# The start's norm from centred squares on ScalarE, image edges set to the mean on two engines, and five pieces of background work moved to other steps

## The chip, the cores and the metric

The kernel runs on one core of a Trainium2 chip. The core has TensorE (PE; its weight loads are listed as PEld), VectorE (DVE), ScalarE (ACT), GpSimd (POOL) and SyncE (SP), which here only issues transfers. Each engine works through its own queue in order, and the engines wait for each other by semaphores. The metric is the device time of one execution in microseconds (us).

## The reference

The input is x, four images of 32 x 32 pixels with 16 channels in float32. Four layers follow each other, each of the form x = x + layer(group_norm(x)). The group norm makes eight groups of two channels and takes mean and variance of an image over all pixels of a group, with 1e-5 added to the variance.

```python
def conv(inputs, M, W, G):               # layers 0, 1 and 3
    first = einsum('ijyx,byxc->bijc', M, inputs)
    shifted = conv3x3(inputs, G)         # for each pixel (i, j) its own filters to f channels, zero padding
    diff = relu(inputs[:, None, None, :, :, :] - shifted)   # b, i, j, y, x, f
    second = einsum('ijyx,bijyxf->bijf', W, diff)
    return first - second

def interval(a, W0, b0, W1, b1, W2, b2): # layer 2
    r = concat(running max, running min of a over the intervals i <= j)
    f = max over k of sigmoid(r[i, k] W0a + r[k, j] W0b + b0)
    f = max over k of sigmoid([f, r][i, k] W1a + r[k, j] W1b + b1)
    return sigmoid([f, r] W2 + b2)
```

Nearly all of the work is `shifted`: for each of the 1024 pixels (i, j) and 16 channels, a 3 x 3 convolution of the whole image.

## The kernel before

The images are worked as two groups g of two images b. Three convolution layers by two groups make six phases, and each phase has eight chunks of 128 pixels (i, j), which lie on the partitions. A chunk has 32 steps, one for each filter f and image b: 1536 steps in all. A step makes 128 x 1024 numbers in a pair of PSUM banks, of which there are four.

**A step** (`first_part`, `second_part`). A float32 product is split in parts[...]. `first_part` issues matmuls with the image copies `ib` and `ia`, then ACT scales the pair of banks (L699). `second_part` issues those with `iyz` and `im9` (named `im` in the profile) and then the reduction on DVE (L716, its output is named `junk`): min with 0, product with the chunk's W, sum. The pair of banks is free when L716 has read it. The first 16 steps ("plain") use float32 weights and the image `raw` itself.

**Weights** (`prep_parts`, L217 to L258). The weights of four filters (a unit) are made ready in a cycle of eight steps: L204 on DVE cuts off the low bits; ACT scales the ninth tap (L176), copies (L237, L241); POOL subtracts and adds (L238, L239, L242) and casts (L244, L246), one after the other; then `prep(u + 1)` subtracts the centre from the next unit's weights (L215, POOL). In the last three steps of the cycle SP issues the copies between halves (L252) and loads a later unit (`load_raw`, L111). L204 of the next unit needs the result of L215.

**Work behind the steps** (`behind`, L768). All the rest is written as generators. `conv_layer` (L743) takes one element of `prep_parts` in each step, and when a counter has run out one element of `behind`. A positive yield in `behind` is a number of steps to wait, `IDLE` and `CALM` wait until the weight cycle is in a step marked so; CALM marks the last three steps of the eight. What is emitted in a step goes into the engines' queues at that place, so the yields set the order of each queue by hand. In phase 0 the work behind is: the rest of the first image's start (`rest_of_start`), group 0's norm, the `constants` of the interval layer, then the next phase's input (`before_conv`), and the loads and matmuls of the first terms. In phases 3 and 4 the interval layer of a group runs behind, and then `before_conv` for the last layer.

**The group norm** (`group_norm`, L334) is a row of small DVE operations with `gap` steps between them, POOL for the centred values and squares, and `inverse_root` (L313): three DVE operations on integers (L319 to L323), then 13 small POOL operations (L326, and three rounds of L328 to L331) and the product with the centred values (L376).

**Placing** (`place`, L291). `split` cuts the image in high and low parts in `temp`. From there SP copies quarters of the partitions into `ia` (eight transfers per image) and `ib` (four).

**The start** (L793 to L903). The first phase's images are loaded as rows shifted by taps (`raw`, slots 0 to 2), not normalised. `XQ` holds the same image with a quarter of the pixels of one channel on each partition. DVE sums it (L842), a matmul makes the group's mean for each row (`to_own`), DVE subtracts it (L856), squares and sums (L859), and a matmul gives the variance. ACT takes the root, DVE the reciprocal (L870). `normal` then normalises slots of `raw` on DVE (L890) or ACT (L887, L888), after which `sides` (L873) multiplies the edges, which lie outside of the image, with 0 or 1 (`kept`); in slot 2 a memset clears the column past the image. `prep_plain` subtracts the centre from the first weights (L215, DVE).

## Time and profile before

| | us |
|---|---|
| median of 3 runs (2476.86 to 2479.35) | 2479.14 |
| the profiled execution | 2478.91 |
| its span | 2477.1 |
| PE busy | 2457.9 |
| DVE busy | 2077.0 |
| ACT busy | 1871.4 |
| POOL busy | 1589.7 |
| ACT scaling, L699, one | 1.008 |
| DVE reduction, L716, one | 1.224 |
| first matmul of the first step begins | 9.61 |

In the profile a line such as "L716 DVE ... junk<-pc,WT 128x1024 f32 x1536 | 1879.6, 1224 | 353.5 <-PE pc L663" gives the source line, the engine, what is written from what, the count, then the busy time of all, the mean of one in ns, and the idle time of the engine ahead of them with what ended it. A line of the list in time begins with start and duration in us; a bracket at its end is the idle time of the engine just before and what ended that. TensorE's granted clock was 1.000 in the profiled execution.

### The profile page before, as it was taken

Reading aid. Unit: us, or ns where it says so; the run is one execution under the profiler, and the core shown is the slowest. Engines: PE = TensorE matmul, PEld = TensorE weight load, DVE = VectorE, ACT = ScalarE, POOL = GpSimd, SP = SyncE. Lnnn points to the kernel's source line nnn. Section 1 sums busy time; section 2 is a strip of 40 time slices with the busy share of each in tenths; the row PEclk is TensorE's granted clock in tenths of the full one; section 3 lists DMA queues with packets and bytes.
Section 4 is the critical chain, followed back from the end, with each engine's and each line's share of the span. In section 5 each row is a group of like instructions: output and inputs, shape, how many; then the busy total and the mean of one; then the engine's idle time right before and its main releaser. Section 6 shows DMA issues by size and latency. Waiting matters only on the chain. (4 is left out here: it accounts for less than half of the span.)

```text
span 2477.1 us, 58166 instructions
## 1 busy us (share of the span) xinstructions
PE 2457.9 (99%) x21906; PEld 2072.9 (84%) x21906; DVE 2077.0 (84%) x3637; ACT 1871.4 (76%) x2159; POOL 1589.7 (64%) x1857
## 2 busy tenths in 40 slices
PE   8999999999999999999999999999999999999999
PEld 5998888888888888888888898888889888888887
DVE  9888878888888888878888888888888888788887
ACT  3778767787777778767777777777777787677776
POOL 4767545676565667555567776776777675555552
PEclk9999999999999999999999999999999999999999
DMA  6457654475444467644454454674445476554442
GB/s 198 128 156 191 188 144 134 131 195 149 135 142 137 137 168 194 190 112 136 137 145 129 126 142 132 174 171 130 129 135 141 119 197 186 154 148 137 137 137 54
DMA packets 97674, 366.92 MB, mean 148 GB/s; under 512 B 26480, under 2 KB 31472, under 8 KB 97392
## 3 DMA queue, kind: packets, MB, share of 16 engines
q1 hardware_dynamic: 96832, 362.79, 53.5%
q8 instruction: 172, 2.82, 0.5%
q14 instruction: 110, 0.90, 0.1%
q10 hardware_dynamic: 432, 0.39, 0.0%
q0 software_dynamic: 128, 0.02, 0.0%
HBM read 199.78 MB, written 1.02 MB: 81 GB/s over the span
## 5 line engine op out<-in xcount | busy, mean ns | idle before, releaser
L716 DVE SCALAR_TENSOR_TENSOR junk<-pc,WT 128x1024 f32<-128x1024 f32 x1536 | 1879.6, 1224 | 353.5 <-PE pc L663 303.8
L699 ACT ACTIVATE pc<-pc 128x1024 f32<-128x1024 f32 x1520 | 1532.2, 1008 | 563.8 <-PE pc L663 530.4
L663 PE MATMUL pc<-ib,parts 64*128 64x512 f32 x6080 | 950.2, 388 | 4.3 <-DVE junk L716 3.0
L663 PE MATMUL pc<-iyz,parts 64*128 64x512 f32 x6080 | 947.2, 387 | 2.3 <-ACT pc L699 1.6
L663 PE MATMUL pc<-ia,parts 64*128 64x496 f32 x6080 | 924.8, 379 | 0.0
L663 PEld LDWEIGHTS pc<-ib,parts 64*128 64x128 f32 x6080 | 582.4, 184 | 109.8 <-DVE junk L716 9.6
L663 PEld LDWEIGHTS pc<-ia,parts 64*128 64x128 f32 x6080 | 585.4, 184 | 106.0
L663 PEld LDWEIGHTS pc<-iyz,parts 64*128 64x128 f32 x6080 | 583.5, 184 | 92.6 <-ACT pc L699 7.3
L663 PE MATMUL pc<-im,W 64*128 64x496 f32 x3072 | 603.2, 384 | 0.0
L238 POOL TENSOR_TENSOR parts<-raw,upper_w 128x512 fp32r<-128x512 f32 x190 | 247.0, 1300 | 497.6 <-DVE upper_w L204 413.1
L663 PEld LDWEIGHTS pc<-im,W 64*128 64x128 f32 x3072 | 296.6, 184 | 56.9 <-issue 3.4
L244 POOL CAST parts<-parts 32x512 fp32r<-32x512 f32 x380 | 231.6, 609 | 39.3 <-ACT parts L241 20.8
L242 POOL TENSOR_TENSOR parts<-parts 128x512 fp32r<-128x512 f32 x190 | 247.0, 1300 | 1.6 <-ACT parts L237 1.5
L246 POOL CAST parts<-upper_w 32x512 fp32r<-32x512 f32 x380 | 233.1, 613 | 22.8
L239 POOL TENSOR_TENSOR W<-W,raw 128x512 fp32r<-128x512 f32 x190 | 247.4, 1302 | 0.4 <-ACT W L176 0.3
L215 POOL TENSOR_TENSOR raw<-raw,ident 128x512 f32<-128x512 f32 x190 | 199.8, 1052 | 73.7 <-DMA raw<-in_g 45.8
L176 ACT ACTIVATE W<-raw,low_w 128x512 fp32r<-128x512 f32 x190 | 136.2, 717 | 1.7 <-DMA raw<-in_g 1.6
L716 DVE DVE_READ_ACCUMULATOR junk<-pc,WT 128x1 f32 x1536 | 127.9, 83 | 0.0
L237 ACT ACTIVATE parts<-upper_w 128x512 fp32r<-128x512 f32 x190 | 118.9, 626 | 7.7 <-DVE upper_w L204 7.5
L241 ACT CAST parts<-upper_w 128x512 fp32r<-128x512 f32 x190 | 116.4, 613 | 0.0
L731 POOL TENSOR_SCALAR acc<-acc 128x32 f32<-128x32 f32 x40 | 15.6, 391 | 136.8 <-DVE junk L716 134.7
L204 DVE TENSOR_SCALAR upper_w<-raw 128x512 int32<-128x512 int32 x190 | 82.4, 433 | 19.0 <-POOL raw L215 18.6
(152 smaller groups left out, 470.4 us busy)
## 6 DMA issues: line engine op xcount, KB each, us to landing
raw<-in_g SPq DMA_DIRECT2D x190, 768.0 KB, 7.1
parts<-parts SPq DMA_DIRECT2D x380, 384.0 KB, 5.0
WT<-in_w SPq DMA_DIRECT2D x48, 512.0 KB, 4.7
MT<-in_mt SPq DMA_DIRECT2D x24, 512.0 KB, 7.3
raw<-xs SPq DMA_DIRECT2D x120, 71.8 KB, 4.1
ib<-temp SPq DMA_DIRECT2D x40, 128.0 KB, 4.4
ia<-temp SPq DMA_DIRECT2D x80, 62.0 KB, 5.6
ib<-first SPq DMA_DIRECT2D x8, 128.0 KB, 2.4
```

Of the source, the lines that this page charges most:

```text
L176: nc.scalar.activation(dst, src, AF.Copy, scale=mask[:, 1:2])
L215: eng.tensor_tensor(raws[u][:, s, at:to], raws[u][:, s, at:to], pick[s][:, f0 + at : f0 + to].unsqueeze(2).to_broadcast([P, to - at, P]), ...
L237: nc.scalar.activation(WD, high, AF.Copy, scale=-EPS)
L238: nc.gpsimd.tensor_tensor(WL, w8, high, ALU.subtract)
L239: nc.gpsimd.tensor_tensor(W9, W9.bitcast(F32), src[:, 2], ALU.add)
L241: nc.scalar.copy(WU, high)
L242: nc.gpsimd.tensor_tensor(WD, WD.bitcast(F32), WL.bitcast(F32), ALU.add)
L244: nc.gpsimd.tensor_copy(WU[hi], WL[lo].bitcast(F32))
L246: nc.gpsimd.tensor_copy(WL[lo], high[hi])
L663: nc.tensor.matmul(ps[:, h, at : at + n], lhsT=w[r], rhs=v[r] if n == NH else v[r][:, :n], start=first and k == 0, stop=k == len(pairs) - ...
L699: nc.scalar.activation(ps, ps, AF.Copy, scale=1.0 + EPS)
L716: nc.vector.scalar_tensor_tensor(junk, ps.rearrange("p h n -> p (h n)"), 0.0, chunks[n], op0=ALU.min, op1=ALU.mult, accum_out=accs[phase][ ...
```

## The change

- **Statistics at the start.** The squares are taken on ACT (`Square` with the bias minus the partition's own mean, and a running sum), and the difference between the own and the group's mean is corrected afterwards (`off`, `off2`). `Square` and `Sqrt` are in two table sets of ACT.
- **Edges.** The edges are set to the mean ahead of the normalisation (times `kept`, plus `fill`, which is the mean or 0), which makes them 0 afterwards. Those of slots 1 and 2 and the centres of the first weights are on POOL, those of slot 0 on DVE. Slot 2 of the second image is normalised on ACT.
- **Placing** copies `ib` first (four transfers), and `ia` with both halves s in one transfer (four). In `before_conv` it follows the differences and `halve_rest`, with other yields.
- **Constants** begin six steps later instead of one, wait four steps after the memset of `rt`, and yield after each block.
- **Interval norm**: gap 1 for 2, a pause until CALM ahead of `inverse_root`, and 4 steps after it for 6.
- **A yield of 2** stands between the second dynamic step ("b") and the left side l2.

```diff
@@ -210,13 +210,16 @@
             return
+        for s in range(2 if u < PLAIN else 1):
+            minus_center(eng, u, s, at, to)
+
+    def minus_center(eng, u, s, at, to):
         f0 = u % NU * FU
-        for s in range(2 if u < PLAIN else 1):
-            eng.tensor_tensor(
-                raws[u][:, s, at:to], raws[u][:, s, at:to],
-                pick[s][:, f0 + at : f0 + to].unsqueeze(2).to_broadcast([P, to - at, P]),
-                ALU.subtract,
-            )
+        eng.tensor_tensor(
+            raws[u][:, s, at:to], raws[u][:, s, at:to],
+            pick[s][:, f0 + at : f0 + to].unsqueeze(2).to_broadcast([P, to - at, P]),
+            ALU.subtract,
+        )
@@ -257,11 +260,14 @@
-    def prep_plain(u, at=0, to=FU, eng=nc.gpsimd):
-        if at == 0:
+    def plain_unit(u):
+        if u not in units:
             units[u] = [None] * 3 + [
...
             ]
+
+    def prep_plain(u, at=0, to=FU, eng=nc.gpsimd):
+        plain_unit(u)
         prep(u, at, to, eng)
@@ -290,15 +296,17 @@
-        ty, tz = (v.bitcast(F32) for v in halves(temp, b))
+        parts = halves(temp.bitcast(F32)[:, :TEMP], b)
         da, db = (v[g].bitcast(F32)[:, :, b] for v in (ia, ib))
+        for lo, hi in QUARTERS:
+            for to, src in zip((lo, hi), parts):
+                nc.sync.dma_start(db[to], src[hi])
         for h, (lo, hi) in enumerate(QUARTERS):
-            for s in range(2):
-                at = HW if s == h else 0
-                for to, src in ((lo, ty), (hi, tz)):
-                    nc.sync.dma_start(da[to, s, :LAST], src[lo, s, at : at + LAST])
-            for to, src in ((lo, ty), (hi, tz)):
-                nc.sync.dma_start(db[to], src[hi])
+            for k, to in enumerate((lo, hi)):
+                at = (2 * k * GB + b) * NH + HW * (1 - h)
+                pitch = GB * NH + HW * (2 * h - 1)
+                src = temp.bitcast(F32)[lo, at : at + 2 * pitch].rearrange("p (s n) -> p s n", s=2)
+                nc.sync.dma_start(da[to, :, :LAST], src[:, :, :LAST])
         yield 1
@@ -331,7 +339,7 @@
-    def group_norm(g, name, dst, gap):
+    def group_norm(g, name, dst, gap, pause=None, behind=6):
@@ -372,9 +380,11 @@
         v = yield from totals(f"v{name}")
+        if pause is not None:
+            yield pause
         rstd = inverse_root(v, name)
         nc.gpsimd.tensor_tensor(pair_view(dst), pair_view(xc), spread(rstd), ALU.mult)
-        yield 6
+        yield behind
@@ -409,17 +419,18 @@
         yield 6 if layer == 2 else 12
-        temp = big.tile([P, 8192], F32R, tag="big", name=f"temp_{g}{layer}")[:, :TEMP]
+        temp = big.tile([P, 8192], F32R, tag="big", name=f"temp_{g}{layer}")
         for b in range(GB):
...
             halve(image(im9[g][:, b], HW), image(raw[:, 2, b], WP), low_x)
-            yield from place(g, b, temp)
             for s in range(2):
                 difference(nc.gpsimd, g, b, s, temp)
+            yield 2
+            halve_rest(image(im9[g][:, b], HW), image(raw[:, 2, b], WP), low_x)
+            yield 2
+            yield from place(g, b, temp)
             yield 1
-            halve_rest(image(im9[g][:, b], HW), image(raw[:, 2, b], WP), low_x)
-            yield 4
@@ -481,7 +492,7 @@
         nc.gpsimd.memset(rt, 0.0)
-        yield 1
+        yield 4
@@ -496,8 +507,8 @@
                 blocks(t[:, q * GB : (q + 1) * GB, :], k, mask2, GB)
+                yield 1
             iv[name] = t.rearrange("p k c -> p (k c)")
-            yield 1
     def interval_layer(g):
@@ -523,7 +534,7 @@
         nc.gpsimd.memset(r[:R, H:], 0.0)
-        yield from group_norm(g, f"i{g}", xi, 2)
+        yield from group_norm(g, f"i{g}", xi, 1, CALM, 4)
@@ -638,6 +649,7 @@
         yield from step("b", ftp, bv[:, 1:2])
+        yield 2
         z = left("l2", iv["f2"])
@@ -772,7 +784,7 @@
             zeros(1)
-            yield 1
+            yield 6
             yield from constants()
@@ -820,66 +832,82 @@
     }
+    beyond = const.tile([P, len(outside)], F32, name="beyond")
     kept = const.tile([P, len(outside)], F32, name="kept")
+    fill = const.tile([P, GB, len(outside)], F32, name="fill")
     keep = {}
     for k, (name, view) in enumerate(outside.items()):
-        keep[name] = kept[:, k : k + 1]
-        nc.vector.tensor_reduce(keep[name], view, axis=AX.X, op=ALU.add)
-    nc.vector.tensor_scalar(kept, kept, -1.0, 1.0, op0=ALU.mult, op1=ALU.add)
+        keep[name] = k
+        nc.vector.tensor_reduce(beyond[:, k : k + 1], view, axis=AX.X, op=ALU.add)
+    nc.vector.tensor_scalar(kept, beyond, -1.0, 1.0, op0=ALU.mult, op1=ALU.add)
     s1 = const.tile([P, 1], F32, name="s1")
-    def first_stats(src, name):
+    def first_stats(by_batch, name):
         ps = bank(f"ps_{name}")
-        by_batch = work.tile([P, GB], F32, tag="by_batch", name=f"by_batch_{name}")
-        nc.vector.tensor_scalar_mul(by_batch, own, src)
         nc.tensor.matmul(
...
+    low_w = rows_mask("low_w", ident.rearrange("p (h w k) -> p w h k", h=2, w=2)[:, 1:2])
+
+    low_p = const.tile([P, 2], F32, name="low_p")
+    nc.vector.tensor_scalar_mul(low_p, low_w, 1.0 / EPS)
+
+    n_own = XQ.shape[1]
     nc.vector.tensor_reduce(s1, XQ, axis=AX.X, op=ALU.add)
+    minus_own = const.tile([P, 1], F32, name="minus_own")
+    nc.vector.tensor_scalar_mul(minus_own, s1, -1.0 / n_own)
+    by_mean = work.tile([P, GB], F32, tag="by_batch", bufs=2, name="by_batch_m0")
+    nc.vector.tensor_scalar_mul(by_mean, own, s1)
     ps = bank("ps_own")
...
     )
-    m = first_stats(s1, "m0")
-    low_w = rows_mask("low_w", ident.rearrange("p (h w k) -> p w h k", h=2, w=2)[:, 1:2])
-    low_x = rows_mask("low_x", ident.rearrange("p (g x k) -> p x g k", g=4, x=2)[:, 1:2])
-    nc.vector.tensor_scalar_mul(low_x, low_x, EPS)
-
-    low_p = const.tile([P, 2], F32, name="low_p")
-    nc.vector.tensor_scalar_mul(low_p, low_w, 1.0 / EPS)
-    mean_own = const.tile([P, 1], F32, name="mean_own")
-    nc.vector.tensor_copy(mean_own, ps[:, :1])
-    nc.vector.tensor_scalar_sub(XQ, XQ, mean_own)
+    m = first_stats(by_mean, "m0")
+    squares = const.tile([P, 256], F32, name="squares")
     s2 = const.tile([P, 1], F32, name="s2")
-    squares = const.tile([P, 256], F32, name="squares")
+    nc.scalar.activation(squares, XQ, AF.Square, bias=minus_own, accum_out=s2)
+
+    plain_unit(0)
+    halve(units[0][3][:, :F0], raws[0][:, 2, :F0], low_p)
+    minus_center(nc.gpsimd, 0, 0, 0, F0)
+    off = const.tile([P, 1], F32, name="off")
+    nc.vector.tensor_tensor(off, minus_own, ps[:, :1], ALU.add)
+    off2 = const.tile([P, 1], F32, name="off2")
     nc.vector.scalar_tensor_tensor(
-        squares, XQ, 1.0, XQ, op0=ALU.mult, op1=ALU.mult, accum_out=s2
+        off2, off, float(n_own), off, op0=ALU.mult, op1=ALU.mult
     )
+    by_var = work.tile([P, GB], F32, tag="by_batch", bufs=2, name="by_batch_v0")
+    nc.vector.scalar_tensor_tensor(
+        by_var, off2.to_broadcast([P, GB]), s2, own, op0=ALU.add, op1=ALU.mult
+    )
+    var = first_stats(by_var, "v0")
     mean0 = const.tile([P, GB], F32, name="mean0")
     minus_mean0 = const.tile([P, GB], F32, name="minus_mean0")
-    var = first_stats(s2, "v0")
     nc.vector.tensor_copy(mean0, m)
     nc.vector.tensor_scalar_mul(minus_mean0, m, -1.0)
+    for b in range(GB):
+        nc.vector.tensor_scalar_mul(fill[:, b], beyond, mean0[:, b : b + 1])
     rstd0 = const.tile([P, GB], F32, name="rstd0")
     nc.scalar.activation(rstd0, var, AF.Sqrt, bias=eps)
-    prep_plain(0, 0, F0, nc.vector)
-    nc.vector.reciprocal(rstd0, rstd0)
-
     def sides(eng, b, slot):
...
         if slot == 2:
-            eng.memset(v[64:, :, HW - 1 : HW], 0.0)
+            at = v[64:, :, HW - 1]
+            eng.tensor_scalar(at, at, mean0[64:, b : b + 1], None, op0=ALU.add)
         for side, at in (
...
             if f"{side}{slot}" in keep:
-                eng.tensor_scalar_mul(at, at, keep[f"{side}{slot}"])
+                k = keep[f"{side}{slot}"]
+                eng.tensor_scalar(
+                    at, at, kept[:, k : k + 1], fill[:, b, k : k + 1], op0=ALU.mult, op1=ALU.add
+                )
@@ -891,14 +919,18 @@
+    sides(nc.vector, 0, 0)
+    sides(nc.gpsimd, 0, 2)
+    minus_center(nc.gpsimd, 0, 1, 0, F0)
+    sides(nc.gpsimd, 0, 1)
+    nc.vector.reciprocal(rstd0, rstd0)
     normal(nc.scalar, 0, 2)
     normal(nc.vector, 0, 0)
-    sides(nc.vector, 0, 0)
+    low_x = rows_mask("low_x", ident.rearrange("p (g x k) -> p x g k", g=4, x=2)[:, 1:2])
+    nc.vector.tensor_scalar_mul(low_x, low_x, EPS)
+    halve(image(im9[0][:, 0], HW), image(raw[:, 2, 0], WP), low_x)
+    normal(nc.vector, 0, 1)
     prep_plain_rest(0, 0, F0)
-    normal(nc.vector, 0, 1)
-    sides(nc.vector, 0, 1)
-    sides(nc.gpsimd, 0, 2)
-    halve(image(im9[0][:, 0], HW), image(raw[:, 2, 0], WP), low_x)
     halve_rest(image(im9[0][:, 0], HW), image(raw[:, 2, 0], WP), low_x)
@@ -908,9 +940,10 @@
         prep_plain_rest(0, F0, FU)
-        for slot in (0, 1, 2):
-            normal(nc.vector, 1, slot)
-            sides(nc.vector, 1, slot)
+        for eng, slot in ((nc.gpsimd, 2), (nc.gpsimd, 1), (nc.vector, 0)):
+            sides(eng, 1, slot)
+        for eng, slot in ((nc.scalar, 2), (nc.vector, 0), (nc.vector, 1)):
+            normal(eng, 1, slot)
         halve(image(im9[0][:, 1], HW), image(raw[:, 2, 1], WP), low_x)
@@ -918,7 +951,7 @@
         yield 2
-        temp = first.bitcast(F32R)[:, used : used + TEMP]
+        temp = first.bitcast(F32R)[:, used:]
         for b in range(GB):
```

A tile of padding is also 48 columns wide instead of 88, and `halves` cuts `temp` to its length itself.

More of the change, by code (lines that the diff above doesn't have):

```diff
@@ L128, in net_kernel @@
     raw = const.tile([P, 3, GB, PITCH], F32, name="raw")
-    const.tile([P, 88], F32, name="pad_parts")
+    const.tile([P, 48], F32, name="pad_parts")
     F0 = 2
@@ L271, in halves @@
     def halves(temp, b):
-        v = temp.rearrange("p (k s b n) -> p k s b n", k=2, s=2, b=GB)
+        v = temp[:, :TEMP].rearrange("p (k s b n) -> p k s b n", k=2, s=2, b=GB)
         return v[:, 0, :, b], v[:, 1, :, b]
```

## The prediction

> **What bounds the kernel now.** I read the totals and the groups by line first, then the list of instructions in time around every place where TensorE (PE) pauses. The totals:

> ```profile
> PE 2457.9 (99%) x21906; PEld 2072.9 (84%) x21906; DVE 2077.0 (84%) x3637; ACT 1871.4 (76%) x2159; POOL 1589.7 (64%) x1857
> ...
> L716 DVE SCALAR_TENSOR_TENSOR junk<-pc,WT 128x1024 f32<-128x1024 f32 x1536 | 1879.6, 1224 | 353.5 <-PE pc L663 303.8
> L215 POOL TENSOR_TENSOR raw<-raw,ident 128x512 f32<-128x512 f32 x190 | 199.8, 1052 | 73.7 <-DMA raw<-in_g 45.8
> L204 DVE TENSOR_SCALAR upper_w<-raw 128x512 int32<-128x512 int32 x190 | 82.4, 433 | 19.0 <-POOL raw L215 18.6
> ```

> PE sets the end: 1536 steps, 1.567 us each (the last matmul of three steps in a row starts at 1562.71, 1564.27 and 1565.84). Nothing in the change alters the matmuls of a step, so it can move only the time at which the first begins and the pauses between steps. Listing the start of the last matmul of each step, I find pauses beyond that pace in some forty places. The change touches few of them, so the forecast is a sum of microseconds.

> How a pause arises is seen at the norm of group 0 before the last layer:

> ```profile
> 1554.90 0.50 POOL L326 TENSOR_SCALAR root_a_c<-root_a_c 128x16 f32<-128x16 f32 x1
> ...
> 1559.87 1.29 POOL L238 TENSOR_TENSOR parts<-raw,upper_w 128x512 fp32r<-128x512 f32 x1
> ...
> 1566.42 1.04 POOL L215 TENSOR_TENSOR raw<-raw,ident 128x512 f32<-128x512 f32 x1
> ...
> 1567.49 0.43 DVE L204 TENSOR_SCALAR upper_w<-raw 128x512 int32<-128x512 int32 x1 [1.38 <-POOL raw L215]
> ```

> The inverse root (Newton: 13 small POOL operations and a product) holds POOL 4.97 us from 1554.90. The weight unit's own POOL work then takes 7.59 us (L238 at 1559.87 to L215's end at 1567.46; 1276.82 to 1284.42 is the same 7.6). DVE's L204 for the next unit waits for L215, and behind it on DVE are queued the reductions L716 that free PSUM. I call lag the start of L716 minus the start of that step's last matmul: about 0.5 on a quiet step, falling 0.2 per step when DVE catches up. Here it peaks at 2.0 and PE loses 0.06. Peaks of 3.83, 3.40 and 2.27 go with losses of 1.49, 1.09 and 0.34. So a loss is the peak less 1.95 to 2.3: that is what four PSUM bank pairs cover.

> The same mechanism, and two others, in the places that the change touches:

> ```profile
> 9.61 3.82 PE L663 MATMUL pc<-raw,first 64*128 64x512 f32 x8 [2.40 <-DVE raw L882]
> 51.14 0.70 PE L663 MATMUL pc<-ib,parts 64*128 64x512 f32 x3 [0.96 <-DMA ib<-first]
> 114.09 0.45 DVE L204 TENSOR_SCALAR upper_w<-raw 128x512 int32<-128x512 int32 x1 [2.41 <-POOL raw L215]
> 1284.45 0.43 DVE L204 TENSOR_SCALAR upper_w<-raw 128x512 int32<-128x512 int32 x1 [2.49 <-POOL raw L215]
> 1643.95 1.04 POOL L215 TENSOR_TENSOR raw<-raw,ident 128x512 f32<-128x512 f32 x1 [7.36 <-DMA raw<-in_g]
> ```

> The first matmul waits for DVE's edges; step 19 waits for the transfer into ib; the other three are late L215s, because of the constants, of the interval norm's Newton, and of a weight load queued on SP behind placing transfers.

> [...] The change needs one more switch, for Square. [...] pairs of matmuls start 0.85 apart until about 14.5 us, 0.43 later[...]. [...] in the trace 128x512 takes 1.05 on POOL (L215), and 128x256 takes 0.41 on DVE and 0.67 on POOL (L376).

> **The change part by part**, against the profiled execution's own 2478.91.

> Start. Now: XQ lands at 3.70, s1 3.72, the subtraction 5.39, squares 5.78 to 6.21, by_batch 6.33, matmul 6.62, rstd on ACT 7.24, reciprocal 7.91, normalise 8.11, edges 8.72 to 9.54, first matmul 9.61. After: Square on ACT needs its table after 3.72, so 5.00; 128x256 on ACT takes about 0.6 (L176 of that size: 0.50), so 5.6; by_var 5.9, matmul 6.2 to 6.5; the W9 product (0.5) and the second table load (1.28) on ACT run to 7.3 and now end last; sqrt 0.26, reciprocal 0.16, normalise 0.58: first matmul at 8.4. Edges and centres run beside this on DVE and POOL; on POOL they end about 9.3, before slot 1 is used. Gain 1.2[...]; both ends 0.5 and 1.2, I take 1.0. [...]

> Small pauses at steps 5 (0.37, DVE normalising image 1, now shared out) and 130 (0.39, placing): 0.76, ends 0 and 0.76; I take it all.

> Placing: 8 transfers for 12, ib first. At 0.6 us of SP per issue, four fewer are 2.4 us, and ib goes four issues sooner where PE waits for it: step 19's 1.25 goes (ends 0.6 and 1.25). ia is now last, but PE wants it 0.45 us after ib in each step. In phase 3 the second image's placing moves from step 1001 to 1009, behind the weight load that it held up (its load was issued at 1633.69, behind twelve placings from 1619.23): steps 1018 and 1019's 1.88 go. It is then still 15 steps ahead of its first use, 23 us.

> Constants: one POOL burst per block becomes one per step: step 59's 1.36 goes. The delay of 14 steps moves all that follows in phase 0, its 8 MT loads on SP and the first terms (7.27 us of PE) too; these only change places, as phase 0 has 256 steps and they end near step 210. But the norm now meets the weight cycle elsewhere, below.

> Interval norms: the pause puts Newton behind L215, in the three steps where POOL has nothing of the weights. Each image lost 1.93 there (1.09 at the Newton, the rest in DVE's backlog with the transposes, which stay and with gap 1 come closer together). Gain 1.1 each, ends 0.5 and 1.7: 2.2.

> The two-step yield after the second step: the matmul ps_l for l2 waits for the transfer of s_b into tables. PE loses 1.56 and 1.68 there and 0.83 for a ps_l that doesn't wait: 0.73 + 0.85 = 1.58 gained. Two steps are 3.1 us, more than the wait.

> Sum of gains: 1.0 + 0.76 + 1.25 + 1.88 + 1.36 + 2.2 + 1.58 = 10.0.

> What is moved, and pays. The yield shifts the next norm (group_norm of layer 2, no pause) by two steps. The order of DVE's instructions after the change shows it: L204 used to follow the root at once; now L204, two L716, the root, six L716, the transpose xt, the next L204. So Newton starts just before L238, and L238 to L215 stand behind it: 12.6 us from Newton's start to L215's end (4.97 + 7.59), with only 6 steps (9.4 us) to the next L204. From the trace: the wait at 1567.49 had a lag of 2.0; Newton starts 2 steps (3.13) later, and 0.42 more because L204 now stands ahead of the root: 2.0 + 3.13 + 0.42 = 5.5, so a loss of 3.25 to 3.6. I take 3.4, and there are two such norms: 6.8. The constants' 14 steps do the same to the norm of group 1 in phase 0: before, its Newton (158.22) stood after the unit's casts and L204 waited only 0.51; now the root comes two L716 after L204, as above. With gap 4 DVE's backlog at the root is 1.2 or so smaller: lag 4.2, loss 1.9 to 2.25, I take 2.1. Sum of losses 8.9. Their cover would be a Newton that ends before L238, and there is none.

> Net: 10.0 - 8.9 = 1.1 faster, 2477.8 on the profiled run's scale. The median shown is 0.23 above that run: forecast 2478.0. About 0.2% (5 us) is what a measurement of this kernel can tell from no change, so the likeliest outcome is no difference.

> **The rivals.**
> One: the late Newtons bite half or not at all. For it: L204 waited 1.80 after the first norm's Newton and PE lost only 0.68. Against: 12.6 us don't fit in 9.4, and the order of both queues is fixed. Time: 2478.0 less 4.5 to 8.9, 2469.1 to 2473.5.
> Two, slower than before: [...]
> Three: the change does less than it says: DVE's closer backlog eats the interval norms' gain (2.2), or the transfers still land late (up to 3.1). Time: 2480 to 2483.

> **How the numbers follow.** The forecast's case 0.55, its own range 2475.5 to 2480 from the ends above; rival one 0.27; rival two 0.06; rival three 0.12. Most of rival one lies below 2474.2, 0.2% under the median; little of two and three lies above 2484.1. So faster 0.27, same 0.67, slower 0.06. The range of 2470.0 to 2482.0 leaves about one in ten on each side.

> **What would show it.** Right: L204 waits of 3.5 or more for L215 near the roots of the last layer's two norms and of group 1 in phase 0, with PE 3 us and 2 us late after them; none near 114, 1284 and 1645; first matmul near 8.4 with two table loads ahead of it; no PE wait for ib at step 19. Wrong: those waits under 2 us, a first matmul after 9.6, or a PE wait for ia at a phase's first step.

## The result, and the profile after

The changed kernel takes 2492.91 us (median of 6, 2491.35 to 2493.68) against 2478.55 before: a ratio of 1.0057 (95% interval 1.0044 to 1.0070), so it is slower by 0.6%. The forecast was 2478.0 and no difference. The gains came as forecast in sum; what the moved work costs was put at 8.9 us and is 23 us.

The totals and the groups that answer to those shown of the kernel before. L728, L218 and L204 are the reduction, the centre of the weights and the cut of their low bits:

```profile
PE 2465.4 (99%) x21906; PEld 2082.3 (84%) x21906; DVE 2076.9 (83%) x3626; ACT 1875.0 (75%) x2164; POOL 1595.3 (64%) x1868
...
L728 DVE SCALAR_TENSOR_TENSOR junk<-pc,WT 128x1024 f32<-128x1024 f32 x1536 | 1879.5, 1224 | 357.5 <-PE pc L675 303.5
...
L218 POOL TENSOR_TENSOR raw<-raw,ident 128x512 f32<-128x512 f32 x190 | 198.0, 1042 | 64.4 <-DMA raw<-in_g 33.0
...
L204 DVE TENSOR_SCALAR upper_w<-raw 128x512 int32<-128x512 int32 x190 | 86.0, 452 | 26.7 <-POOL raw L218 26.0
```

PE is busy 7.5 us longer with the same matmuls, so some of them ran slower; and DVE's idle time ahead of L204 for L218 is 26.0 us instead of 18.6, although the waits near 114, 1284 and 1645 are gone.

Listing the start of each step's last pair of matmuls as in the prediction, I get these differences. They add to 13.9 us; the span grew by 13.6 (2477.1 to 2490.7), and the rest lies in pauses of under 0.2.

| where | lost before | lost after | difference | forecast |
|---|---|---|---|---|
| up to step 16 | (46.42) | (46.08) | -0.34 | -1.37 |
| steps 19, 20 (ib before, ACT after) | 1.29 | 0.56 | -0.73 | -1.25 |
| steps 59 to 63 (constants) | 1.42 | 0 | -1.42 | -1.36 |
| interval norms, 795 to 802 and 1051 to 1058 | 3.90 | 0.48 | -3.42 | -2.2 |
| l2 matmuls, both | 3.24 | 1.68 | -1.56 | -1.58 |
| 1018, 1019 (placing) | 1.88 | 0 | -1.88 | -1.88 |
| 107, 108 (Newton, group 1 of phase 0) | 0 | 3.72 | +3.72 | +2.1 |
| 75, and 130 to 150 | 0.39 | 1.87 | +1.48 | -0.39 |
| 963 to 973 and 1219 to 1228 (last layer's Newtons) | 0.72 | 10.15 | +9.43 | +6.8 |
| 983 to 996 and 1247 to 1252 | 0 | 8.67 | +8.67 | none |

(Up to step 16 the time of the last matmul stands instead of a loss.) L204's wait at group 1's norm is 3.22 us, a little under the 3.5 that the prediction named; PE stops for 1.83 after it.

The list in time at the first of the last layer's norms, to be read against the four lines of the prediction:

```profile
1558.21 0.25 POOL L334 TENSOR_SCALAR root_a_c<-root_a_c 128x16 f32<-128x16 f32 x1 [4.19 <-DVE root_t_c L328]
...
1562.91 1.30 POOL L241 TENSOR_TENSOR parts<-raw,upper_w 128x512 fp32r<-128x512 f32 x1
...
1569.48 1.04 POOL L218 TENSOR_TENSOR raw<-raw,ident 128x512 f32<-128x512 f32 x1
...
1570.55 0.43 DVE L204 TENSOR_SCALAR upper_w<-raw 128x512 int32<-128x512 int32 x1 [3.89 <-POOL raw L218]
...
1572.17 0.72 PE L675 MATMUL pc<-ib,parts 64*128 64x512 f32 x4 [2.95 <-DVE junk L728]
...
1574.11 1.06 PE L675 MATMUL pc<-ib,parts 64*128 64x512 f32 x4
```

This is the forecast stall: 12.31 us from Newton's start to L218's end (12.6 forecast), L204 3.89 late, PE stopped for 2.95. What was not forecast is the last line: the same four matmuls that take 0.62 take 1.06. The windows around it (stretch, its length, busy time of PE, PEld, DVE, ACT and POOL, then the granted clock, the DMA share and GB/s):

```profile
1570.00:1572.00 2.00, 0.00 (x0) 0.00 (x0) 1.45 (x2) 0.99 (x2) 1.41 (x2) 1.00 0.78 160
1572.00:1574.00 2.00, 1.82 (x14) 1.54 (x16) 1.73 (x5) 1.70 (x3) 2.00 (x3) 0.89 0.92 237
1574.00:1576.00 2.00, 2.00 (x12) 1.57 (x12) 1.87 (x3) 0.40 (x1) 1.88 (x3) 0.50 0.88 243
1576.00:1578.00 2.00, 2.00 (x16) 1.59 (x16) 0.93 (x3) 1.01 (x1) 1.43 (x3) 0.75 0.88 192
1578.00:1580.00 2.00, 2.00 (x22) 1.64 (x20) 1.64 (x3) 1.27 (x2) 0.48 (x1) 1.00 0.22 28
```

After the pause the granted clock is at 0.50 from 1573.57 to 1576.99, and PE, now the slow one, loses more (1.38 in step 972 alone, when the lag was down to 1.28). The second stall is 23 steps later. SP's queue and what waits for it:

```profile
1570.64 1.14 SPq L111 DMA_DIRECT2D raw<-in_g  x1
1571.83 7.87 SPq L406 DMA_DIRECT2D xs<-xt  x8
...
1588.57 10.77 SPq L417 DMA_DIRECT2D raw<-xs  x14
...
1600.71 1.20 SPq L111 DMA_DIRECT2D raw<-in_g  x1
...
1610.81 1.04 POOL L218 TENSOR_TENSOR raw<-raw,ident 128x512 f32<-128x512 f32 x1 [5.96 <-DMA parts<-parts]
...
1611.88 1.41 DVE L204 TENSOR_SCALAR upper_w<-raw 128x512 int32<-128x512 int32 x1 [2.83 <-POOL raw L218]
```

The image on its way to the next layer's input goes out as eight transfers `xs<-xt` and comes back as 24 `raw<-xs`. Here the eight stand right behind a weight load and take SP 7.87 us; before, they stood ahead of the copies and the load and took 3.78. The gathers follow late, then the weight load of 1600.71; it landed at 1610.68, and POOL and DVE waited for it. (The view names the copies `parts<-parts` as what ended POOL's wait, but these landed at 1605.04 and 1612.32. The load landed 0.13 before L218 began, as at the other waits of L218 here.) PE's two pauses that follow are also followed by a clock of 0.50, from 1614.54 to 1617.95.

Of the 8.67 in the table's last row, 0.47 is at step 983, where PE waits for the copies `parts<-parts`. The kernel without the two-step yield, below, has 0.33 there, so this small part is not of the second stall.

At the start, the change did what it says:

```profile
4.04 1.28 ACT L872 ACT_TABLE_LOAD   x1 [4.04 <-DMA XQ<-in_xq]
...
5.33 0.51 ACT L872 ACTIVATE squares<-XQ,minus_own 128x256 f32<-128x256 f32 x1
...
6.35 1.28 ACT L895 ACT_TABLE_LOAD   x1
...
7.65 0.26 ACT L895 ACTIVATE rstd<-ps_v,eps 128x2 f32<-128x2 f32 x1
...
8.91 2.08 PE L675 MATMUL pc<-raw,first 64*128 64x512 f32 x4 [2.08 <-issue]
```

Each table load takes 1.28, the next activate begins 0.01 to 0.02 later, and the second load began 0.02 after the activate before it. It was the same in the kernel before at 330.10: the activate ahead of L445's load ended at 330.08, the load took 1.28, and the next activate began at 331.39. So these switches cost 1.28 each and, but for the 0.01 to 0.02 on either side, nothing more that shows.

### The profile page after: what moved, and what is told of

Its sections match the earlier page's. It is cut to its first block, busy times and chain, and to the rows that moved or that the text cites. A ratio compares the mean times of both kernels' runs of the same rounds, so it can differ in the third digit from the quotient of the medians.

```text
span 2490.7 us, 58101 instructions
## 1 busy us (share of the span) xinstructions
PE 2465.4 (99%) x21906; PEld 2082.3 (84%) x21906; DVE 2076.9 (83%) x3626; ACT 1875.0 (75%) x2164; POOL 1595.3 (64%) x1868
## 4 chain that ended last, share of the span: by engine, by line
PE 92%; DMA 2%; DVE 2%; POOL 2%; issue 1%; ACT 1%; DVEq 0%; POOLq 0%; ACTq 0%; SPq 0%
PE pc L675 91%; DMA raw<-in_g 2%; DVE junk L728 2%; PE pf L450 1%; ACT pc L711 1%; DMA first<-in_g 0%; POOL raw L218 0%; DMA parts<-parts 0%; POOL parts L241 0%; POOL parts L245 0%; ACT temp L291 0%; POOL parts L249 0%; POOL parts L247 0%; PE ps_l L584 0%; PE ps_r L599 0%
## 5 line engine op out<-in xcount | busy, mean ns | idle before, releaser
L728 DVE SCALAR_TENSOR_TENSOR junk<-pc,WT 128x1024 f32<-128x1024 f32 x1536 | 1879.5, 1224 | 357.5 <-PE pc L675 303.5
L218 POOL TENSOR_TENSOR raw<-raw,ident 128x512 f32<-128x512 f32 x190 | 198.0, 1042 | 64.4 <-DMA raw<-in_g 33.0
L176 ACT ACTIVATE W<-raw,low_w 128x512 fp32r<-128x512 f32 x190 | 136.2, 717 | 4.8 <-DMA raw<-in_g 4.7
L728 DVE DVE_READ_ACCUMULATOR junk<-pc,WT 128x1 f32 x1536 | 127.7, 83 | 0.0
L204 DVE TENSOR_SCALAR upper_w<-raw 128x512 int32<-128x512 int32 x190 | 86.0, 452 | 26.7 <-POOL raw L218 26.0
```

The costliest lines, as they stand in the source:

```text
L176: nc.scalar.activation(dst, src, AF.Copy, scale=mask[:, 1:2])
L218: eng.tensor_tensor(raws[u][:, s, at:to], raws[u][:, s, at:to], pick[s][:, f0 + at : f0 + to].unsqueeze(2).to_broadcast([P, to - at, P]), ...
L728: nc.vector.scalar_tensor_tensor(junk, ps.rearrange("p h n -> p (h n)"), 0.0, chunks[n], op0=ALU.min, op1=ALU.mult, accum_out=accs[phase][ ...
```

## The experiments

### Taking the two-step yield out of the changed kernel

```diff
         yield from step("b", ftp, bv[:, 1:2])
-        yield 2
         z = left("l2", iv["f2"])
```

> The changed kernel without the two-step yield after the second dynamic step. The changed kernel loses, in each of the last layer's two norms, about 5 us after the late Newton (steps 971 to 973 and 1227 to 1228) and about 4 us some 23 steps later (994 to 996 and 1250 to 1252). Theory A, the shift alone does both, by putting Newton ahead of the weights' POOL work and the image gathers ahead of a weight load on SP: both go, 18.1 us less, and 1.6 us come back at the l2 matmuls: about 2476.4 us. Theory B, the second stall belongs to the new order of placing: only the first goes, about 2484.5 us.

Measured: 2477.44 us, ratio to the kernel before 0.9997 (0.9988 to 1.0005). The list of steps has neither stall of the last layer's norms (steps 963 and 971 lose 0.33 and 0.14, 994 and 1250 nothing) and 1.65 and 1.70 at the l2 matmuls. Theory A holds: one line of two steps costs the changed kernel 15.5 us. The new placing, which is still in, does not make the second stall by itself.

### The two-step yield alone in the kernel before

> The kernel before with the two-step yield alone. The l2 matmuls gain 1.6 us. Theory two stalls from one line: the first stall of 5.1 us comes in both norms, and a second one 20 to 30 steps later, of 4 us or so, in place of the old 1.9 at 1018: about 2493 us. Theory one stall: 2486.5 us. If the shift were harmless: 2477 us.

Measured: 2494.53 us, ratio 1.0057 (1.0037 to 1.0076). In the profiled execution steps 964 to 973 lose 5.24 and 1221 to 1228 5.00 (L204 waits behind Newton, PE stops for 3.3 twice), and 983 to 1003 and 1242 to 1259 lose 4.9 and 3.6 (without the 0.4 of steps 1002 and 1258, which the kernel before has too). So this line has both stalls without any other part of the change, and by itself makes up the slowdown of the whole.

### One Newton round for three, every queue's order kept

```diff
-        for _ in range(3):
+        for _ in range(1 if name in ("c02", "c12") else 3):
```

> The changed kernel with one Newton round instead of three in the two norms ahead of the last layer (it leaves out two thirds of the root's iteration, 8 POOL operations of about 0.31 us, 2.5 us), and with the order of every queue as it is. The first stall's lag falls from 5.0 to about 2.5, its loss from 5.1 to about 0.7 us, with no slow clock. Theory follow-up (the stall 23 steps later comes of the first one): it goes as well, about 2476 us in all. Theory gathers (14 image gathers ahead of a weight load on SP are enough): the stalls of 4 us at 994 and 1250 stay, about 2484 us.

Measured: 2486.59 us in one execution. The first stall went as forecast: the lag peaks at 2.68 and 0.74 is lost at 971, 0.71 at 1227. The second stayed: 4.1 us at 994 to 1003, 5.5 at 1239 to 1259 (again without that 0.4). L204 near 1609 still waits 3.37 for L218. So the second stall does not come of the first. But that the number of gathers sets it, as the expectation named it, is refuted by the next two kernels. In this trace the eight `xs<-xt` are issued 1.2 us behind the weight load of 1569.11, which landed at 1578.01; the first of them lands at 1578.59, 8.3 us after its issue, and the last at 1579.95. In the kernel before they land 1.6 to 1.9 us after their issues.

### Newton in the quiet part in every norm ahead of a convolution

```diff
-        yield from group_norm(g, f"c{g}{layer}", xn, 1 if layer == 2 else 4)
+        yield from group_norm(g, f"c{g}{layer}", xn, 1 if layer == 2 else 4, CALM, 4)
```

> The changed kernel with the pause until CALM (and 4 steps after) in the norms ahead of the convolutions too, so that their Newton stands behind L218; the two-step yield stays. The stalls at 107 to 108 (3.7 us), 971 to 973 (5.1) and 1227 to 1228 (5.1) go in every theory: 13.9 less. Theory A1, the stall 23 steps later is set by how many image gathers SP issues between two weight loads (14 there, 16 here): it stays, about 2479 us. Theory A2, it follows from the first stall, which made SP's transfers late: it goes too, about 2471 us.

Measured: 2471.11 us, ratio 0.9967 (0.9957 to 0.9976): faster than both kernels. The list in time at the same norm:

```profile
1556.56 1.04 POOL L218 TENSOR_TENSOR raw<-raw,ident 128x512 f32<-128x512 f32 x1
...
1557.72 1.14 SPq L111 DMA_DIRECT2D raw<-in_g  x1
...
1558.65 0.25 POOL L334 TENSOR_SCALAR root_a_c<-root_a_c 128x16 f32<-128x16 f32 x1 [1.04 <-DVE root_t_c L328]
...
1561.19 0.42 DVE L204 TENSOR_SCALAR upper_w<-raw 128x512 int32<-128x512 int32 x1
...
1564.51 4.37 SPq L406 DMA_DIRECT2D xs<-xt  x8
```

Newton now runs behind L218, L204 doesn't wait, and no step from 952 to 993 loses anything. All the Newton stalls are gone (107, 971, 1227), and 994 and 1250 lose 0.37 and 0.38, with 16 gathers between two weight loads where the changed kernel has 14. So the count is not what makes the loads late. Here too the eight `xs<-xt` come after a weight load in SP's order, but 6.8 us after it (it landed at 1564.74), and they land 1.9 to 2.4 us after their issues. The edit has two parts, the pause and 4 steps for 6; the next kernel has the second part alone, in the last layer's norms.

### The eight transfers ahead of the weight load

The changed kernel with 4 steps instead of 6 behind the norm of layer 2 and nothing else.

> The changed kernel with 4 steps instead of 6 after the norm ahead of the last layer, so that the eight transfers xs<-xt stand ahead of the weights' copies and load on SP again, as in the kernel before; Newton stays where the change put it. In the changed kernel they stand 1.2 us behind a weight load and land after 5 to 8 us instead of 2. Theory xs (this is what makes the loads some 20 steps later late): the stalls at 994 and 1250 (4.0 and 4.2 us) go, those at 971 and 1227 stay: about 2484.5 us. Theory Newton alone: all stalls stay, 2493 us.

Measured: 2485.14 us, ratio 1.0021 (1.0013 to 1.0030).

```profile
1564.77 3.79 SPq L406 DMA_DIRECT2D xs<-xt  x8
...
1570.29 1.04 POOL L218 TENSOR_TENSOR raw<-raw,ident 128x512 f32<-128x512 f32 x1
...
1571.36 0.43 DVE L204 TENSOR_SCALAR upper_w<-raw 128x512 int32<-128x512 int32 x1 [4.13 <-POOL raw L218]
...
1571.39 1.20 SPq L111 DMA_DIRECT2D raw<-in_g  x1
...
1572.99 0.73 PE L675 MATMUL pc<-ib,parts 64*128 64x512 f32 x4 [2.92 <-DVE junk L728]
```

The first stall is as in the changed kernel (4.81 at 971 and 972, 4.85 at 1227 to 1229); of the second, 0.42 at 996 is left and nothing at 1250. This and the last two kernels part the two stalls: the first is Newton ahead of the weights on POOL, and the second comes with the order on SP that has the eight small transfers close behind a weight load.

One thing is not parted. When the eight move, the gathers move too: 14 and then 10 of them stand between weight loads before and here, 10 and then 14 in the kernels with the second stall, 6, 16 and 2 in the one with the quiet Newtons. The stall goes with how late one weight load is. Counted in steps of the same trace, it is issued at 986.8 to 987.1 in the kernels with the full stall (changed, one round, constants as before, two-step yield alone) and at 983.3 to 985.6 in those without (before, no yield, quiet Newtons, this one). With all norms quiet, below, it is issued at 986.1, and 0.83 is lost at 994 and 995. (At the second norm it is 1243.1 to 1243.5 against 1239.4 to 1242.2.) The late landing of the eight fits as a part of that: in the changed kernel and in the one with quiet Newtons they are issued at the same step, 970.6 and 970.4, and the first gather follows at 974.8 and at 974.0. How much the gathers' own place adds was not tried.

### The constants as before

> The changed kernel with the constants as before (begin after one step, one yield after the memset, none inside the blocks). If the 14 steps of delay put group 1's Newton of phase 0 in the way, the stalls at 107 to 108 (3.7 us) and the added loss at 130 to 150 (1.3 us) go, and step 59's 1.4 us comes back: about 2489.3 us. If the constants' place has nothing to do with it, only step 59 comes back: about 2494.3 us.

Measured: 2489.23 us, ratio 1.0046 (1.0031 to 1.0061). The stall at 107 and 108 is gone, and step 59's is back with 1.36. That part of the shift was the cause, as forecast. Its profiled execution is 3.5 us above its median. In it the last layer's norms lost 12.5 instead of 10.1, because the clock stayed at half for 6.83 us at each of them, not 3.41; and 1.53 at step 111 and 1.23 at 314 and 315, which the changed kernel did not lose, are not explained.

### Pauses of TensorE by the size of the hold-up

```diff
+                held = HOLD.get(32 * n + at, 0)          # {362: 4, 378: 5, ... 474: 11}
+                if held:
+                    c = steps[at - 1][1] * C + steps[at - 1][0]
+                    nc.gpsimd.tensor_scalar_mul(squares[:, :1], accs[phase][:, t, c : c + 1], 1.0)
+                for _ in range(held):
+                    nc.gpsimd.tensor_scalar_mul(squares, squares, 1.0)
```

> The kernel before with POOL held up at eight quiet places of phase 1 (every 16 steps from step 362), ahead of L238 and after a reduction, by 4, 5, ... 11 operations of 128x256 on a dead tile (about 0.67 us each, so 2.7 to 7.4 us). Lag peaks of about 1.6 to 6.3 us. Theory clock, a TensorE pause of 2 us or more lets its clock fall to half for some 3 us: the loss follows the peak less 2 up to a pause of about 2, then jumps by 1 to 1.5 us, with a granted clock of 0.5 behind the pause. Theory backlog, the clock is not at fault: the loss is the peak less about 2 all along, and the clock stays at 1.00. Total about 2493 us for clock, 2487 for backlog.

Measured: 2523.30 us in one execution, 44.8 more than the kernel before; the losses at the eight places add to 44.4. From one operation to the next it took 0.93 us, not 0.67, so the series reaches further. The pause runs from the last matmul's start ahead of it to the next one's.

| operations | peak lag | PE's pause | loss | loss less (peak - 1.94) |
|---|---|---|---|---|
| 4 | 2.74 | under 0.9 at once | 0.80 | 0 |
| 5 | 3.67 | 1.81 | 1.73 | 0 |
| 6 | 4.60 | 2.74 | 4.26 | 1.6 |
| 7 | 5.53 | 3.66 | 5.18 | 1.6 |
| 8 | 6.48 | 4.59 | 6.09 | 1.6 |
| 9 | 7.39 | 5.53 | 7.94 | 2.5 |
| 10 | 8.35 | 6.45 | 8.98 | 2.6 |
| 11 | 9.20 | 7.31 | 9.46 | 2.2 |

The granted clock behind the pauses of 1.81, 2.74 and 6.45 us, in the windows (columns as above):

```profile
641.00:644.00 3.00, 2.47 (x22) 2.07 (x24) 2.73 (x5) 2.46 (x3) 3.00 (x3) 1.00 0.99 215
...
669.00:671.00 2.00, 1.74 (x8) 1.46 (x10) 1.73 (x5) 1.17 (x2) 2.00 (x3) 0.57 0.98 246
...
796.00:798.00 2.00, 1.16 (x6) 0.97 (x8) 1.87 (x3) 1.75 (x3) 2.00 (x2) 0.50 1.00 234
```

Theory clock holds. Up to a pause of 1.8 us, PE loses its pause; from 2.7 on it loses 1.6 to 2.6 us more, with the granted clock at 0.50 behind the pause.

The traces also show when it fell. In each of the 14 profiles here, between start and end, the granted clock changes only at times a whole number of 3.41 us apart, and is at half for one or two such stretches, 3.41 or 6.83 us. In the changed kernel it fell at 191.18, 1573.57, 1614.54, 1990.00 and 2030.96, each time for 3.41. By these numbers one stretch at half costs an estimated 1.7 us of full speed (half of 3.41), about the 1.6 of the table. I cut each trace into these stretches up to the last steps. Among those at full clock, each of the 20 in which PE is idle for 1.79 us or more is followed by one at half, and none with 1.50 or less. Five of the 20 are the changed kernel's, idle for 1.8 to 2.3 us; the next most idle one of that trace, with 0.94 from 1566.75, is not followed by one. Group 1's norm is a good case, because the same pause of 2.2 us fell differently in two kernels, the changed one (first fence) and the one with one Newton round (second; columns as above, PE's busy time first):

```profile
187.76:191.18 3.42, 1.58 (x16) 1.02 (x14) 1.91 (x4) 1.59 (x3) 2.75 (x4) 1.00 0.61 128
191.18:194.59 3.41, 3.41 (x20) 2.70 (x18) 2.87 (x5) 1.50 (x2) 3.29 (x4) 0.50 0.90 249
```

```profile
189.59:193.01 3.42, 1.99 (x18) 1.67 (x20) 3.15 (x6) 2.85 (x4) 3.06 (x3) 1.00 0.97 221
193.01:196.42 3.41, 3.41 (x34) 2.86 (x32) 3.14 (x6) 2.25 (x3) 3.15 (x5) 1.00 0.96 245
```

The first lost 3.72 at steps 107 and 108, the second 2.14.

### The start alone, and the placing alone

> The kernel before with the new start alone (squares on ScalarE, edges at the mean, both engines). First matmul at 8.7 to 8.9 instead of 9.6 and everything else as before: 0.5 to 1.2 us less. [...]

Measured: one execution, 2481.09 us, within what the kernel before itself showed on that chip (2475.97 to 2484.05). Its first matmul begins at 8.53, step 16 at 45.29. The start varies from one execution to the next, so I compare all profiles: step 16's last pair is at 45.29 to 46.42 in eight profiles with the new start (middle 45.8), and at 46.30 to 48.41 in four with the old one (middle 46.8; the kernels with slower steps, below, are left out). The gain is about 1 us. The two groups overlap by 0.1, so its size is rough; the first matmul of the first step begins at 8.34 to 8.91 in the eight and at 9.12 to 10.78 in the four.

> The kernel before with the new placing alone (eight transfers, ib first, after the differences). Step 19 loses 0.5 to 0.6 instead of 1.3, and the stall of 1.9 at 1018 to 1019 goes: about 2.6 less, 2476 us. If the new placing brings the stalls at 994 and 1250 of the changed kernel, those appear here: about 2484 us.

Measured: 2539.96 us, 60 more than the kernel before, and not by any stall: every step took 1.613 us instead of 1.567. I first took this for a fault of that one execution.

> The kernel before with the new placing alone, a second time: in its first execution each step took 1.613 us instead of 1.567 from the first to the last, so its time says nothing about the change. In it steps 19 and 1018 lost nothing. Theory as before: 2.6 to 3.1 us less, about 2476 us.

Measured: 2540.02 us, ratio 1.0239 (1.0224 to 1.0254). It was no accident. With the placing I had also taken over the change's narrower padding tile (48 columns for 88), without the small tiles that the new start adds.

> The new placing alone, this time with the unused tile ahead of the working tiles 88 columns wide as in the kernel before (the kernel of the last run had the changed kernel's 48, without the new small tiles of the start, so that all tiles after it lay 160 bytes lower per partition; each step took 1.613 us there). If the place of the tiles in memory is what made every step slower, a step takes 1.567 us again and the total is 2.6 to 3.1 us under the kernel before, about 2476 us. If the placing itself makes the steps slower (other operands, other transfers), it stays at 2540 us.

Measured: 2477.63 us, ratio 0.9994 (0.9985 to 1.0003), a step 1.567 us again. The two kernels differ in that one number:

```diff
-    const.tile([P, 48], F32, name="pad_parts")
+    const.tile([P, 88], F32, name="pad_parts")
```

The groups of matmuls in the last but one kernel and, in the second fence, in the last (busy time, mean ns of one):

```profile
L666 PE MATMUL pc<-ib,parts 64*128 64x512 f32 x6080 | 962.1, 392 | 0.6 <-DVE junk L719 0.3
...
L666 PE MATMUL pc<-ia,parts 64*128 64x496 f32 x6080 | 947.2, 389 | 0.0
```

```profile
L666 PE MATMUL pc<-ib,parts 64*128 64x512 f32 x6080 | 948.9, 388 | 3.7 <-DVE junk L719 2.9 <-DMA parts<-parts 0.5
...
L666 PE MATMUL pc<-ia,parts 64*128 64x496 f32 x6080 | 923.2, 379 | 0.0
```

From the start of one pair of matmuls to the next it is 227 to 235 ns in the slow one and 220 to 227 in the other (medians from 1100 to 1260 us; seven pairs make a step). The width of that unused tile moves all tiles behind it, so I take the place of the operands to be the cause; how it acts was not shown, since only these two widths were tried. As for the placing: steps 19 and 20 lose 0.32 instead of 1.29 and 1018 nothing, but 983 to 989, 1006 and 1262 lose 2.1 in all and the l2 matmul at 947 another 0.9, so that alone it brings nothing that can be measured.

### The first norm's Newton in the quiet part too

> The variant with the quiet Newtons, with the same pause in the very first norm (group 0 in phase 0) as well. The loss of 0.66 us at step 51 goes, if that Newton is its cause; what follows in phase 0 comes some steps later, which can cost up to 1 us. About 2470.5 us, against 2471.1.

Measured: 2470.88 us, ratio 0.9961 (0.9946 to 0.9976). Step 51's 0.66 is gone, and 0.83 at steps 994 and 995 stands where the other had 0.37; against the kernel with the other quiet Newtons (2471.11) the time can't be told apart.

## Why the prediction was wrong

**The side was wrong for a size and an omission, not for a gain that failed.** The gains were put at 10.0 and are 9.4 in the table. That the sum fits is partly luck, since two parts were too high and one too low. The parts agree within 0.1 at the constants, the l2 matmuls and 1018. The interval norms gave 1.2 more, because DVE's backlog, which was to stay, went too (1.93 to 0.24 per image). Step 19's was too high by 0.5. The start was forecast at 1.0 for the norm and 0.37 for step 5, and it is about 1.0 over all profiles. Step 5 gained nothing that can be seen: in the changed kernel's profile its pause is 0.73 instead of 0.37, and over all profiles it varies from 0 to about 1.2 with the old start and the new.

**"A loss is the peak less 1.95 to 2.3" was the mis-sized term.** The peaks were right: 5.5 forecast and 5.18 measured for the last layer's norms, 4.2 and 4.07 for group 1's. But the rule came from peaks of up to 3.83 and was applied beyond them. (Its spread is a slip in reading: taken over all steps of a stall, the losses of the kernel before are 1.88, 1.47, 0.34 and 0.06, each its peak less 1.93 to 1.95.) With 1.94 the rule gives 3.24 and 2.13, and the stalls lost 1.6 more each, about what one stretch of 3.41 us with the clock at half costs; where the clock stayed up, in the kernel with one round, the stall of group 1 lost 2.14. The prediction had no term for the clock behind a stall. In these traces it fell to 0.50 behind pauses of 2.7 to 3.3 us each time, behind one of 2.2 in three of four kernels (at group 1's norm), and behind two pauses of 1.1 and 1.5 in a row at 1611 to 1614. No fixed length of pause fits this; the idle time in one stretch of 3.41 us, as counted above, fits all of them. So 3.4 per norm became 4.7 (9.43 for both instead of 6.8), and 2.1 became 3.72.

**The step that was missing: SP.** The prediction followed the two-step shift through DVE and POOL and stopped there. The same shift took the eight transfers `xs<-xt` from ahead of a weight load to right behind it. The second stall, 8.2 us (8.67 less the 0.47 of step 983), came with this order, as the kernels show that part it from the first stall: it stays when Newton is short, and goes when the eight transfers stand two steps earlier. In the changed kernel the clock is at half for 3.41 us in each of its two parts (from 1614.54 and from 2030.96), which by the estimate above can account for 1.7 of each. How it divides between the late landing of the eight and the gathers' new place between the weight loads is not shown. Seven of the eight then took 5.00 to 8.03 us instead of 1.6 to 1.9: the load, issued at 1570.64, landed at 1579.38, and all eight landed behind it in the order of their issue, from 1579.86 to 1581.26. That the load held them up is read from these landings; how it did is not shown. The kernel before has such late landings too: seven gathers, issued from 1570.06 behind the load of 1568.75 (landed at 1577.29), landed after 3.8 to 7.4 us and cost nothing, because no weight load came too late behind them. With both terms at their measured size, 10.0 gained and 21.8 lost, the forecast would have been on the right side.

**Steps 130 to 150** were to gain 0.39 but lost 1.3 more. In the kernel with quiet Newtons only 0.37 of it is left, and without the shift of the constants 0.9 (125 and 130), so it follows from the stall at 107 in large part; the rest I did not separate.

**The rivals.** One (late Newtons bite half) is refuted: they cost 1.5 times what was forecast. Two (slower than before) is refuted for the start: the two table loads took 1.28 each, and the first matmul began at 8.91 instead of 9.61. Three is refuted in its first half (DVE's closer backlog eats the interval gain): that gain was the one above its forecast. In its second half (transfers still land late) it is refuted for ib at step 19 and for the weight load of 1018, but a transfer that it did not name, a weight load, came late elsewhere.

## What to carry to other kernels

Where yields set the order by hand, moving one block by two steps moves everything behind it, so follow it through every queue, the transfer queue too: look there for small transfers that come to stand close behind a large one, and for the loads that follow them. A TensorE stall is not a linear cost: in these traces, once PE was idle for 1.8 us of a 3.41 us stretch, 1.6 us or more was lost on top, with the granted clock at 0.50. And a long chain of small operations belongs where its engine has nothing that others wait for: here a pause ahead of the root, with two steps fewer behind it, was worth 21.8 us to the changed kernel, and took it under the kernel before (0.9967).
